# K for pairs of token tiles by seven half-size products, with phase 1 reordered

## The chip, the cores and the metric

The kernel runs on one core of one Trainium2 chip. The metric is device time in microseconds (us), the median of several runs. A core has five engines with a queue each: TensorE (PE, matmuls; its weight loads are shown as PEld), VectorE (DVE), ScalarE (ACT), GpSimd (POOL) and SyncE (SP, which here only issues transfers). Matmuls write to PSUM, a small memory of eight banks of 128 x 512 fp32; VectorE and ScalarE read it back. All data are fp32, and one fp32 product shows up as two matmul instructions in the profile.

## The reference

Two batches of 1024 tokens, model width 512. With `xn` the layer-normed input:

```python
Q = elu(xn @ wq.T + bq) + 1;  K = elu(xn @ wk.T + bk) + 1;  V = xn @ wv.T + bv    # 16 heads of 32
KV = K^T V per head;  K_sum = sum of K over the tokens
attn = (Q KV / (Q K_sum + 1e-8)) @ wo.T + bo
logits = xn @ W_router      # top 2 of 8 experts, weights from sigmoid scores
ffn = (silu(gate) * up) @ W_down, each with a shared and eight routed low-rank corrections
out = x + attn + ffn
```

## The kernel before, in words

Tokens lie in 16 tiles of 128 (`NTILE`), eight to a batch. A batch's `xnT` (features on partitions, tokens along the free axis) is kept in SBUF in four quarters: two halves of the features times two groups of 512 tokens. The program is written engine by engine in emission order: on TensorE, VectorE, ScalarE and GpSimd each instruction runs in the order in which the code emits it, so an instruction that waits holds up everything behind it on its engine. Transfers are issued from SP's queue, whose order the framework chooses.

Most large products use Winograd's form of Strassen's scheme: a 2 x 2 block product by seven half-size products, with sums of weight blocks and of token blocks made beforehand. For the queries (`query_unit`, from line 541) the sums of tokens come from `token_sums` (line 424: four subtractions of 1024 elements for a batch) and those of the weights from `query_weight_sums`.

Phase 1 is the loop from line 472, one tile a round. For tile i it:

- transposes the next tile's normed rows (`transpose_x`, line 262: four TensorE transposes, two ScalarE copies into `xnT`);
- norms the tile after that on VectorE (`norm`), from moments (`moments`, line 233) and a reciprocal standard deviation with one Newton step (`deviations`, line 239, with a Sqrt on ScalarE), and loads a new tile of x into a ring of four;
- computes K and the router's logits (`project_k`, line 271): four chunks of 128 features, each times two halves of the weights of 256 and 264 columns, plainly, no seven-product form. ScalarE copies the logits out; VectorE adds the bias and takes the minimum with 0, ScalarE takes the exp, VectorE finishes with `elu_k` (line 296);
- adds the previous tile's share to the Gram matrix (`accumulate`, line 299): four products xn^T K of 128 x 512 into four banks `pg` that stay open for a whole batch; GpSimd adds K into `ksum`.

The Gram matrix gives KV later, in `Finish` (line 309): copies out, `sums` (sums of `ksum`, and `ksr` from bank `pr`), `values` and `outputs`. For batch 0 it runs among the tiles of batch 1, for batch 1 as hooks of the first query unit. `route` (line 377) turns the logits of four tiles into expert weights. The four other banks rotate among `pt` and the two `pk`.

At the end of each group the query weight sums and the token sums are fed into VectorE's queue at fixed rounds (lines 522 to 528). `query_unit` computes seven products for two chunks with the banks `pqx`, `pqu`, `pqv`; ELU of a result is a VectorE operation, a relu and an exp on ScalarE, and a deferred add that `flush` emits. Phase 3 (from about 249 us) is the feed-forward part; `xdiff`, a difference of two halves of the low-rank activations, is made by GpSimd at its start (line 1255), and `inner_weight_sums` and `token_sums_23` are GpSimd's too.

Of the kernel before, what the change touches and what calls it, by code (L numbers as in the profile page):

```python
# [37 lines left out]
def layer_kernel(  # L38
# [56 lines left out]

    def by_chunk(w):
        return w.rearrange("(c p) n -> p c n", p=P)
# [42 lines left out]
    def load_x(i):  # L140
        x_sb[i] = x_ring[:, i % 4, :]
        nc.sync.dma_start(out=x_sb[i], in_=x[ts(i, P), :])
# [13 lines left out]
    for i, a in enumerate((a_gate, a_up)):  # L156
        nc.sync.dma_start(out=a_in[:, :, i, :], in_=by_chunk(a))
    ad_sb = const.tile([P, FULL + 1, LR], F32, name="ad_sb")
    nc.sync.dma_start(out=ad_sb[:, 0:FULL, :], in_=by_chunk(a_down[0 : FULL * P, :]))
    nc.sync.dma_start(out=ad_sb[0:REST, FULL, :], in_=a_down[RC, :])  # L160
# [52 lines left out]

    mv = p1.tile([P, NTILE, nc.vector.BN_AGGR_DIM], F32, name="mv")
# [5 lines left out]
    ps_pool = [pool(psum1, "ps1", bufs=4, space=PSUM)]  # L220
# [3 lines left out]
    def bank(name, shape=None):  # L224
        tag = next(tags) if tags else "ps"
        return ps_pool[0].tile(shape or [P, TB], F32, tag=tag, name=name)


    warm = bank("warm", [P, NC, P])
# [9 lines left out]
    def deviations(first, n):  # L239
        sl = slice(first, first + n)  # L240
        ve = p1w.tile([P, TPB], F32, tag="ve", name=f"ve{first}")[:, 0:n]
        nc.vector.tensor_scalar_add(ve, mv[:, sl, 1], LN_EPS)
        sd = p1w.tile([P, TPB], F32, tag="sd", name=f"sd{first}")[:, 0:n]
        nc.scalar.activation(sd, ve, AF.Sqrt)
        r0 = p1w.tile([P, TPB], F32, tag="r0", name=f"r0{first}")[:, 0:n]
        nc.vector.reciprocal(r0, sd)

        nt = p1w.tile([P, TPB], F32, tag="nt", name=f"nt{first}")[:, 0:n]
        nc.vector.tensor_mul(nt, r0, r0)
        nc.vector.tensor_mul(nt, nt, ve)  # L250
        nc.vector.tensor_scalar(nt, nt, -0.5, 1.5, ALU.mult, ALU.add)
        nc.vector.tensor_mul(rstd[:, sl], r0, nt)
# [3 lines left out]
    def norm(i):  # L256
        xns[i] = p1w.tile([P, D], F32, tag="xn", name=f"xn{i}", bufs=4)
        nc.vector.tensor_scalar(
            xns[i], x_sb[i], mv[:, i, 0:1], rstd[:, i : i + 1], ALU.subtract, ALU.mult
        )  # L260

    def transpose_x(i):
        pt = bank(f"pt{i}", [P, NC, P])
        for c in range(NC):
            nc.tensor.transpose(pt[:, c, :], xns[i][:, ts(c, P)], ident)
        for k in range(2):
            nc.scalar.copy(xnT[i // TPBATCH][k][:, :, ts(i % TPBATCH, P)], pt[:, 2 * k : 2 * k + 2, :])  # L267

    lg = {}

    def project_k(i, between=None):

        cols = ts(i % TPBATCH, P)
        pk = [bank(f"pk{i}_{s}", [P, HD + s * E]) for s in range(2)]
        for c in range(NC):
            if c == NC - 1 and between:
                between()
            for s in range(2):
                nc.tensor.matmul(  # L279
                    pk[s], xt(i // TPBATCH, c, cols), wk_sb[:, c, s * HD : (s + 1) * HD + s * E],  # L280
                    start=(c == 0), stop=(c == NC - 1),
                )
        g, t = i // TPB, i % TPB
        if t == 0:
            lg[g] = p2.tile([P, TPB, E], F32, tag="lg", name=f"lg{g}", bufs=2)
        nc.scalar.copy(lg[g][:, t, :], pk[1][:, HD:])

        kt = p1w.tile([P, D], F32, tag="kt", name=f"kt{i}", bufs=3)
        for s in range(2):
            nc.vector.tensor_add(kt[:, ts(s, HD)], pk[s][:, 0:HD], bk_sb[:, ts(s, HD)])  # L290
        ek = p1w.tile([P, D], F32, tag="ek", name=f"ek{i}")
        nc.vector.tensor_scalar_min(ek, kt, 0.0)
        nc.scalar.activation(ek, ek, AF.Exp)
        return kt, ek
# [4 lines left out]
    def accumulate(i, pg, ksum, xn, kt):  # L299

        j = i % TPBATCH
        if j == 0:
            nc.gpsimd.tensor_copy(ksum, kt)
        else:
            nc.gpsimd.tensor_add(ksum, ksum, kt)  # L305
        for m in range(NC):
            nc.tensor.matmul(pg[m], xn[:, ts(m, P)], kt, start=(j == 0), stop=(j == TPBATCH - 1))  # L307

    class Finish:
# [6 lines left out]
        def bank(self, name, shape=None):  # L316
            if self.b == 0:
                return bank(name, shape)
# [9 lines left out]
        def sums(self):  # L328
# [4 lines left out]
            pr = self.bank(f"pr{self.b}")  # L333
            nc.tensor.matmul(pr, ones, self.ksum, start=True, stop=True)
# [7 lines left out]

            self.ksr = p1.tile([P, NC, P], F32, tag="ksr", name=f"ksr{self.b}")
# [79 lines left out]

    def token_sums(b):
# [3 lines left out]
        ts_ = {1: b11, 2: b21, 3: b22}  # L428
        tsum.append(ts_)
        t12 = slot(10 if b == 0 else 9, [2, 2, TB], f"t12_{b}")  # L430
        tsum_pair.append(t12)
        ts_[5], ts_[6] = t12[:, 0], t12[:, 1]
        nc.vector.tensor_sub(ts_[5], b12, b11)
        yield
        nc.vector.tensor_sub(ts_[6], b22, ts_[5])
        yield
        t34 = slot(11, [2, 2, TB], "t34_0") if b == 0 else tsp.tile([P, 2, 2, TB], F32, tag="t2", name="t34_1")
        ts_[7], ts_[4] = t34[:, 0], t34[:, 1]
        nc.vector.tensor_sub(ts_[7], b22, b12)
        yield  # L440
        nc.vector.tensor_sub(ts_[4], b21, ts_[6])
# [20 lines left out]
    for i in range(2):  # L462
        moments(i, 1)
        deviations(i, 1)
        norm(i)
        load_x(i + 4)
    transpose_x(0)
    wq_sums, sums0, sums1 = query_weight_sums(), token_sums(0), token_sums(1)
    late = None
    fin = []  # L470
    ws = {}
    for i in range(NTILE):
        if i == 0:
            wv_sb = slot(4, [NC, D], "wv_sb")
            nc.sync.dma_start(out=wv_sb, in_=by_chunk(wvT))
        if i == 1:
            wo_sb = slot(5, [NC, D], "wo_sb")
            nc.sync.dma_start(out=wo_sb, in_=by_chunk(woT))
        if i == 2:
            wq_sb = slot(6, [NC, D], "wq_sb")  # L480
            nc.sync.dma_start(out=wq_sb, in_=by_chunk(wqT))
        if 0 < i < NTILE - 1:
            transpose_x(i + 1)
        if i == 0:
            moments(2, 1)
            deviations(2, 1)
        if i + 2 < NTILE:
            norm(i + 2)
        if i + 6 < NTILE:
            load_x(i + 6)  # L490
        kt, ek = project_k(i, (lambda: transpose_x(1)) if i == 0 else None)
        if i == 0:
            moments(3, 1)
        more = i % 2 == 1 and i + 3 < NTILE
        if more:
            moments(i + 3, 2)
        elu_k(kt, ek)
        if more:
            deviations(i + 3, 2)
        if i == 0:  # L500
            deviations(3, 1)
        n = i // TPB - 1
        if i % TPB == 0 and n >= 0:
            ws[n] = route(n)
        if i == 1:
            gather_factors()
            make_spread()
        t = i - TPBATCH
        if t == 3:
            fin[0].outputs((0, 1))  # L510
        if t == 4:
            fin[0].outputs((2, 3))
        if late is not None:
            accumulate(*late)
            if t == 0:
                fin.append(Finish(0, late[1], late[2]))
                fin[0].copies()
# [1008 lines left out]
```

## Time and profile before

| | us |
|---|---|
| median of 3 runs | 747.81 (746.48 to 747.92) |
| the profiled execution | 746.78 |
| its span, first to last instruction | 745.0 |
| TensorE busy | 733.7 |
| VectorE busy | 465.7 |
| ScalarE busy | 201.0 |
| GpSimd busy | 159.1 |
| phase 1, from the first K product to the first query product | 8.2 to 132.4 |
| first query unit | 132.4 to 169.7 |

A row of a timeline has the start, the length, the engine, the line of the kernel, the operation, what it writes and reads (buffer numbers left out), the shape, and the number of instructions that were merged; in brackets the idle time before it and what ended it. A length is that of the whole row: instructions of one engine overlap a little, so the distance from start to start is the better measure of what one costs. The mean granted TensorE clock was 0.999 of full speed.

### The profile page before, as it was taken

How to read it: one execution, taken by the hardware profiler on the slowest of the kernel's cores; microseconds unless marked ns; L12 is line 12 of the kernel's file. 1: busy time of each engine (PE TensorE's matmuls, PEld its weight loads, DVE VectorE, ACT ScalarE, POOL GpSimd, SP SyncE). 2: the span in 40 equal slices, each digit the busy share in tenths (PEclk: the TensorE clock that was granted, in tenths of full speed). 3: DMA queues.
4: the chain of work that ended last, by engine and by line, in shares of the span. 5: the costliest groups of instructions: out<-in, count | busy, mean ns of one | idle time of the engine just before them, and what ended most of it. 6: DMA issues, size and time to landing. Idle time of an engine off the chain costs nothing.

```text
span 745.0 us, 8741 instructions
## 1 busy us (share of the span) xinstructions
PE 733.7 (98%) x3106; PEld 494.8 (66%) x3106; DVE 465.7 (63%) x967; ACT 201.0 (27%) x432; POOL 159.1 (21%) x201
## 2 busy tenths in 40 slices
PE   8999999999999999999999999999999999999997
PEld 6666666454333566666566666666788888888886
DVE  5666665455677788878888888878952602703303
ACT  4445352533333333333333343243000000000000
POOL 3211212012000790311212213524601003101001
PEclk9999999999999999999999999999999999999999
DMA  9811001007313101211210210352465316323001
GB/s 232 231 29 43 15 0 58 0 1 185 121 29 126 33 4 57 84 33 57 86 53 33 85 58 29 127 183 97 162 189 196 125 45 209 124 68 112 19 1 57
DMA packets 52733, 63.29 MB, mean 85 GB/s; under 512 B 9425, under 2 KB 39505, under 8 KB 52434
## 3 DMA queue, kind: packets, MB, share of 16 engines
q1 hardware_dynamic: 52018, 62.46, 26.6%
q10 hardware_dynamic: 672, 0.28, 0.3%
q8 instruction: 24, 0.39, 0.2%
q14 instruction: 19, 0.16, 0.1%
HBM read 40.97 MB, written 21.76 MB: 84 GB/s over the span
## 4 chain that ended last, share of the span: by engine, by line
PE 87%; DVE 8%; ACT 2%; issue 1%; DMA 0%; POOL 0%; DVEq 0%; ACTq 0%
PE po L1383 25%; PE ab L956 15%; PE b L1016 7%; PE pk L279 7%; PE pg L307 6%; PE pqu L559 3%; PE ph L1406 3%; PE x L956 2%; PE pqv L559 2%; PE pxa L638 2%; PE pr L850 2%; PE b L1011 2%; DVE r L1038 2%; PE x L1011 1%; PE pv L355 1%
## 5 line engine op out<-in xcount | busy, mean ns | idle before, releaser
L1383 PE MATMUL po<-wd,f 128*128 128x256 f32 x560 | 122.5, 380 | 0.3 <-DVE xr L1452 0.2
L1383 PEld LDWEIGHTS po<-wd,f 128*128 128x128 f32 x560 | 106.0, 190 | 16.4 <-issue 2.1
L1016 PE MATMUL b<-t,w 128*128 128x512 f32 x160 | 83.2, 602 | 0.0
L279 PE MATMUL pk<-wk_sb,xnT 128*128 128x256 f32 (+1 forms) x256 | 59.3, 384 | 1.4 <-ACT xnT L267 1.4
L307 PE MATMUL pg<-kt,xn 128*128 128x512 f32 x128 | 57.5, 592 | 0.0
L1413 DVE TENSOR_TENSOR had<-ph,wT 64x256 f32<-64x256 f32 x8 | 3.4, 422 | 80.7 <-PE ph L1406 80.5
L279 PEld LDWEIGHTS pk<-wk_sb,xnT 128*128 128x128 f32 x256 | 47.4, 190 | 8.8 <-ACT xnT L267 2.1
L1430 ACT COPY a<-po 128x512 f32<-128x512 f32 x4 | 2.3, 585 | 185.1 <-PE po L1383 185.1
L1383 PE MATMUL po<-kvo,f 128*128 128x256 f32 x224 | 49.4, 381 | 0.0
L1038 POOL TENSOR_TENSOR r<-r,r 128x512 f32<-128x512 f32 x20 | 30.2, 1531 | 83.0 <-DVE t L1038 83.0
L1383 PEld LDWEIGHTS po<-kvo,f 128*128 128x128 f32 x224 | 42.3, 190 | 7.1 <-issue 1.2
L956 PE MATMUL ab<-ti,wi 128*128 128x256 f32 x180 | 45.4, 379 | 0.0
L956 PEld LDWEIGHTS ab<-ti,w 128*128 128x128 f32 x140 | 25.2, 189 | 29.7 <-DVE r L984 9.3
L1038 DVE TENSOR_TENSOR r<-r,r 128x512 f32<-128x512 f32 x60 | 44.1, 776 | 0.0
L956 PEld LDWEIGHTS ab<-ti,wi 128*128 128x128 f32 x180 | 34.2, 190 | 13.1 <-issue 4.8
L956 PE MATMUL ab<-ti,w 128*128 128x256 f32 x140 | 41.2, 388 | 0.7 <-DVE r L984 0.4
L307 PEld LDWEIGHTS pg<-kt,xn 128*128 128x128 f32 x128 | 24.4, 190 | 25.2 <-issue 23.6
L989 ACT COPY r<-ab 128x256 f32<-128x256 f32 x50 | 18.6, 372 | 71.8 <-PE ab L956 71.8
L305 POOL TENSOR_TENSOR ksum<-ksum,kt 128x512 f32<-128x512 f32 x14 | 19.9, 1423 | 77.4 <-DVE kt L297 47.7
L1016 PEld LDWEIGHTS b<-t,w 128*128 128x128 f32 x160 | 29.3, 190 | 10.4 <-issue 5.9
L966 ACT COPY r<-ab 128x256 f32<-128x256 f32 x50 | 18.6, 373 | 49.1 <-PE ab L956 46.9
L984 DVE TENSOR_TENSOR r<-r,ab 128x256 f32<-128x256 f32 x50 | 20.9, 418 | 17.2 <-ACT r L981 16.7
(240 smaller groups left out, 1259.2 us busy)
## 6 DMA issues: line engine op xcount, KB each, us to landing
h_dram<-h SPq DMA_DIRECT2D x40, 256.0 KB
f<-h_dram SPq DMA_DIRECT2D x20, 512.0 KB
x_ring<-in_x_dram SPq DMA_DIRECT2D x16, 256.0 KB
q_dram<-qt SPq DMA_DIRECT2D x16, 256.0 KB
f<-q_dram SPq DMA_DIRECT2D x8, 512.0 KB
xr<-in_x_dram SPq DMA_DIRECT2D x8, 512.0 KB
out_dram<-xr SPq DMA_DIRECT2D x16, 256.0 KB
w<-in_w_gate_dram SPq DMA_DIRECT2D x10, 256.0 KB
```

The lines of the kernel that those rows point to most:

```text
L279: nc.tensor.matmul(pk[s], xt(i // TPBATCH, c, cols), wk_sb[:, c, s * HD : (s + 1) * HD + s * E], start=(c == 0), stop=(c == NC - 1),)
L305: nc.gpsimd.tensor_add(ksum, ksum, kt)
L307: nc.tensor.matmul(pg[m], xn[:, ts(m, P)], kt, start=(j == 0), stop=(j == TPBATCH - 1))
L559: nc.tensor.matmul(banks[c], wqs[p][:, k, ts(c, P)], tsum[b][p][:, k, :], start=(start and k == 0), stop=(k == 1), skip_group_check=True,)
L956: nc.tensor.matmul(out, w, t, start=start, stop=True, skip_group_check=True)
L966: nc.scalar.copy(self.r[0][:, H0], self.ua)
L984: nc.vector.tensor_add(self.r[1][:, H1], self.r[1][:, H1], self.lo)
L1011: nc.tensor.matmul(banks[m], bgu_sb[rows, cols], act[rows, :], start=starts[m], stop=True, skip_group_check=True)
L1016: nc.tensor.matmul(pb[m], ws[m][:, A_OF[p], ts(k, P)], tsum[b][p][:, k, :], start=start, stop=True, skip_group_check=True)
L1038: eng.tensor_add(to[m], t[m], v[m])
L1383: nc.tensor.matmul(ps[p][:, q, :], lhsT, rhs, start=start, stop=stop, skip_group_check=True)
L1406: nc.tensor.matmul(ph[g * ER : (g + 1) * ER, :], a, f[:, g, :], start=(n == 0), stop=(n == len(chunks) - 1), skip_group_check=True,)
```

## The change

Tiles are taken in pairs: tile t of token group 0 and tile t of token group 1 of a batch (`TILES`). The first pair is still computed with `project_k`; the seven others with `k_pair`, where the two tiles are the two token blocks, the two halves of the features the inner blocks, and the two halves of K's columns the outer blocks. Seven products of 128 x 256 (or 264, with the logits' columns) over 256 features go into three banks, `ua`, `x` and `lo`; the bank `ua` is written by product 1 and then added to by products 6, 5 and 3, and VectorE reads it between them. Each product is two fp32 matmuls. The four sums of K's weights are made by GpSimd at the start (`key_weight_sums`), the four sums of tokens by VectorE for each pair (`pair_token_steps`); for batch 0 they are written where the query unit expects `token_sums(0)`, which goes away.

Around it: the Gram products, transposes, norms and moments are interleaved with the products in a new order; the Newton step works column by column; each Sqrt is followed by a dummy Exp; the logits are copied by VectorE; the loads of `a_in`, `ad_sb`, `wq`, `wv` and `wo` are held back by a small VectorE memset (`hold`) until given places in the order; factor and spread copies on GpSimd come in pair 3; routing comes in pair 7 and in the first query unit; in `query_unit` the copies of u2 come before the ELU of the first results; `xdiff` is made before phase 3.

```diff
+    TILES = [b * TPBATCH + g * TPB + t for b in range(NBATCH) for t in range(TPB) for g in range(2)]
...
+    def hold(v):
+        nc.vector.memset(v, 0.0)
...
-    for i, a in enumerate((a_gate, a_up)):
-        nc.sync.dma_start(out=a_in[:, :, i, :], in_=by_chunk(a))
+    def load_factors():
+        hold(a_in[:, 0, 0, 0:1])
+        for i, a in enumerate((a_gate, a_up)):
+            nc.sync.dma_start(out=a_in[:, :, i, :], in_=by_chunk(a))
+        hold(ad_sb[:, 0, 0:1])
...
+    def variances(first, n):
...
         nc.scalar.activation(sd, ve, AF.Sqrt)
+        if first > 2:
+            nc.scalar.activation(idle[:, 1:2], idle[:, 0:1], AF.Exp)
...
-        nc.vector.tensor_mul(nt, r0, r0)
-        nc.vector.tensor_mul(nt, nt, ve)
+        cols = [slice(k, k + 1) for k in range(n)]
+        for c in cols:
+            nc.vector.tensor_scalar(nt[:, c], r0[:, c], r0[:, c], ve[:, c], ALU.mult, ALU.mult)
         nc.vector.tensor_scalar(nt, nt, -0.5, 1.5, ALU.mult, ALU.add)
-        nc.vector.tensor_mul(rstd[:, sl], r0, nt)
+        for k, c in enumerate(cols):
+            nc.vector.tensor_scalar_mul(rstd[:, first + k : first + k + 1], nt[:, c], r0[:, c])
...
+    def key_weight_sums():
+        a11, a12 = (wk_of[0, k][:, :, 0:HD] for k in range(2))
+        a21, a22 = wk_of[1, 0], wk_of[1, 1]
+        s1, s2, s3, s4 = (wks[:, k, :, 0:HD] for k in range(4))
+        nc.gpsimd.tensor_add(s1, a21, a22)
+        nc.gpsimd.tensor_sub(s2, s1, a11)
+        nc.gpsimd.tensor_sub(s3, a11, a21)
+        nc.gpsimd.tensor_sub(s4, a12, s2)
...
+    def pair_token_steps(m):
...
+        nc.vector.tensor_sub(t34[:, 0], b22, b12)
+        yield
+        nc.vector.tensor_sub(t12[:, 0], b12, b11)
+        nc.vector.tensor_sub(t12[:, 1], b22, t12[:, 0])
+        nc.vector.tensor_sub(t34[:, 1], b21, t12[:, 1])
...
+    def add_keys(late):
+        (na, _, ksum, ka), (_, _, _, kb) = late
+        if na % TPBATCH == 0:
+            nc.gpsimd.tensor_add(ksum, ka, kb)
+        else:
+            for kt in (kb, ka):
+                nc.gpsimd.tensor_add(ksum, ksum, kt)
...
+    def k_pair(m, late, hooks={}):
...
+        product(2, x_, True)
+        product(7, lo, True)
+        product(1, ua, True)
...
+        if m == 1:
+            moments(4, 2)
+            variances(4, 2)
+        nc.vector.tensor_copy(la, ua[:, HD:])
+        nc.vector.tensor_add(ka[:, HI], ua[:, 0:HD], bk_sb[:, HI])
+        nc.vector.tensor_add(ka[:, HI], ka[:, HI], x_[:, 0:HD])
+        nc.vector.tensor_add(la, la, x_[:, HD:])
+        if m == 1:
+            reciprocals()
+        norms()
+        at("n")
+        add_keys(late)
+        if m > 1:
+            accumulate(*l_a)
+        else:
+            accumulate(*l_b, ms=range(3))
+        product(6, ua)
+        nc.vector.tensor_add(ka[:, LO], ua[:, 0:HD], bk_sb[:, LO])
+        at("a")
+        if ahead:
+            transpose_x(2 * m + 2)
+        accumulate(*l_b, ms=range(2) if m > 1 else ())
+        more = 2 * m + 4 < NTILE
+        if more:
+            moments(2 * m + 4, 2)
+            variances(2 * m + 4, 2)
+        product(5, ua)
+        nc.vector.tensor_add(kb[:, LO], ua[:, 0:HD], bk_sb[:, LO])
+        nc.vector.tensor_add(kb[:, LO], kb[:, LO], lo)
+        if ahead:
+            transpose_x(2 * m + 3)
+        accumulate(*l_b, ms=range(2, 4) if m > 1 else (3,))
+        at("b")
+        if m > 1 and ahead:
+            pair_token_sums(m + 1)
+        product(4, lo)
+        product(3, ua)
+        nc.vector.tensor_add(ka[:, LO], ka[:, LO], lo)
+        sums = pair_token_steps(2) if m == 1 else iter(())
+        next(sums, None)
+        ea = elu_min(ka, f"ek{na}") if m > 1 else None
+        nc.vector.tensor_add(kb[:, HI], ua[:, 0:HD], bk_sb[:, HI])
+        nc.vector.tensor_copy(lb, ua[:, HD:])
+        ea = ea or elu_min(ka, f"ek{na}")
+        list(sums)
+        elu_k(ka, ea)
+        eb = elu_min(kb, f"ek{nb}")
+        if more:
+            reciprocals()
+        elu_k(kb, eb)
...
+    hooks = {
+        (1, "b"): [lambda: load_weights(wq_sb, wqT)],
+        (2, "n"): [lambda: next(wq_sums), load_factors],
+        (2, "b"): [lambda: next(wq_sums), lambda: load_weights(wv_sb, wvT)],
+        (3, "n"): [lambda: next(wq_sums), lambda: next(wq_sums)],
+        (3, "b"): [lambda: load_weights(wo_sb, woT), lambda: pair_token_sums(0), gather_factors, make_spread],
+        (4, "b"): [lambda: fin.append(Finish(0, pg, ksum)), lambda: fin[0].copies()],
+        (5, "a"): [lambda: fin[0].sums(), lambda: fin[0].chunk_sums()],
+        (6, "a"): [lambda: fin[0].values()],
+        (6, "b"): [lambda: fin[0].outputs((0,))],
+        (7, "a"): [lambda: routed(0), lambda: fin[0].outputs((1,))],
+        (7, "b"): [lambda: fin[0].outputs((2, 3))],
+    }
...
+        if m == 0:
...
+            ka = project_k(0, [[(0, "lo"), (1, "ua")]], lambda: transpose_x(1))
+            variances(3, 1)
+            key_weight_sums()
+            ea = elu_min(ka, "ek0")
+            reciprocals()
+            norm(3)
+            load_x(7)
+            kb = project_k(1, [[(1, "x"), (0, "pt")]])
+            transpose_x(2, "lo")
+            elu_k(ka, ea)
+            eb = elu_min(kb, "ek1")
+            transpose_x(3, "ua")
+            pair_token_sums(1)
+            elu_k(kb, eb)
...
-        for c in two:
-            elu(c, 0)
         hook("P1")
         product(6, up, start=False)
         u2 = [q[c + NPQ, 0] for c in two]
         for c in two:
             nc.scalar.copy(u2[c], up[c])
-        flush()
+        for c in two:
+            elu(c, 0)
...
-        ws[3] = route(3)
-        accumulate(*late)
-        fin.append(Finish(1, late[1], late[2]))
+        add_keys(late)
+        for args in late:
+            accumulate(*args)
+        for n in (1, 2):
+            routed(n)
+        fin.append(Finish(1, pg, ksum))
...
+        nc.gpsimd.tensor_sub(xdiff[b], xa[b][:, 0:TB], xa[b][:, TB:BT])
```

## The prediction

> **What bounds the kernel now.** I read the page first (busy shares, the chain that ended last), then the timeline of each engine over the first 190 us, where the edits lie, and last the waits.
>
> ```profile
> PE 733.7 (98%) x3106; PEld 494.8 (66%) x3106; DVE 465.7 (63%) x967; ACT 201.0 (27%) x432; POOL 159.1 (21%) x201
> PE 87%; DVE 8%; ACT 2%; issue 1%; DMA 0%; POOL 0%; DVEq 0%; ACTq 0%
> ```
>
> TensorE is busy all the time, so a saved matmul is saved time only as long as the next one finds its operands and its bank ready. TensorE's timeline shows the old rhythm and the two holes that matter here.
>
> ```profile
> 49.37 0.60 PE L265 MATMUL pt<-ident,xn 128*128 128x128 f32 x4
> 49.81 3.67 PE L279 MATMUL pk<-wk_sb,xnT 128*128 128x256 f32 x16
> 53.32 3.60 PE L307 MATMUL pg<-kt,xn 128*128 128x512 f32 x8
> 56.75 0.60 PE L265 MATMUL pt<-ident,xn 128*128 128x128 f32 x4
> ...
> 82.28 3.34 PE L279 MATMUL pk<-wk_sb,xnT 128*128 128x264 f32 x14 [0.60 <-ACT xnT L267]
> ...
> 148.89 3.70 PE L559 MATMUL pqu<-t,wq_sums 128*128 128x512 f32 x8 [0.90 <-ACT qt L595]
> ...
> 722.16 12.36 PE L1383 MATMUL po<-kvo,f 128*128 128x256 f32 x56
> ```
>
> From start to start: four transposes 0.44, K of one tile 3.51 (16 instructions, two for each fp32 product), its share of the Gram 3.43 (8 instructions, 0.43 each): 7.38 us a tile, without idle. A 256-wide instruction takes 0.218 (12.2 us over 56, L1383).
>
> What could stop the new order is VectorE, which must empty the bank between products, and who holds VectorE up. Two timelines side by side, VectorE:
>
> ```profile
> 54.34 0.54 DVE L258 TENSOR_SCALAR xn<-x_ring,mv,rstd 128x512 f32<-128x512 f32 x1
> 59.25 1.49 DVE L258 TENSOR_SCALAR xn<-x_ring,mv,rstd 128x512 f32<-128x512 f32 x1
> 64.52 0.17 DVE L246 RECIPROCAL r<-sd 128x2 f32<-128x2 f32 x1 [0.27 <-ACT sd L244]
> 64.72 0.88 DVE L249 TENSOR_TENSOR nt<-r 128x2 f32<-128x2 f32 x1
> ```
>
> and GpSimd:
>
> ```profile
> 58.88 1.58 POOL L305 TENSOR_TENSOR ksum<-ksum,kt 128x512 f32<-128x512 f32 x1 [5.67 <-DVE kt L297]
> 64.32 1.27 POOL L305 TENSOR_TENSOR ksum<-ksum,kt 128x512 f32<-128x512 f32 x1 [3.86 <-DVE ve L242]
> ```
>
> The same norm takes 0.54 alone and 1.49 beside a GpSimd add; both delayed operations end just after that add does. The reciprocal beside it is not delayed. Last, ScalarE's table loads:
>
> ```profile
> 22.02 1.28 ACT L244 ACT_TABLE_LOAD   x1 [1.68 <-DVE ve L242]
> ...
> 33.20 1.28 ACT L244 ACT_TABLE_LOAD   x1
> 34.77 0.20 ACT L244 ACTIVATE sd<-ve 128x2 f32<-128x2 f32 x1 [0.28 <-DVE ve L242]
> ```
>
> A Sqrt needs a load of 1.28. Sometimes it starts before the Sqrt's input is there (33.20), sometimes only after (22.02).
>
> **What it removes from TensorE.** Pair 0 is still computed plainly. Seven pairs go from 32 instructions to 28, and the 264-wide ones stay 128 in number, so 7 x 4 = 28 instructions of width 256 go: 28 x 0.218 = 6.1 us, all on the bounding engine. A new pair is 6.15 (28 products) + 6.87 (16 Gram) + 0.87 (8 transposes) = 13.9 us on TensorE, against 14.8.
>
> The first two norms lose one small VectorE operation each (0.195 from start to start in the first timeline microseconds): TensorE starts 0.2 earlier. The 0.60 at 82.28 came from ScalarE's table loads ahead of a transpose copy in an order that is gone. The 0.90 at 148.89 came from relu and exp standing ahead of the u2 copies; now the copies come first, and the two later routings fit in VectorE's idle 5.2 us before 141.75 plus the 3.4 us of the extra Gram tile. Without that cover the 0.9 comes back. Together 1.7.
>
> **What it adds: the loop of a pair.** The copies of the logits move from ScalarE to VectorE, the four long token sums of batch 0 (1.22 each, L433 to L441) become four short ones in every pair. I lay VectorE's queue out in emission order. Step A is the add that empties ua after product 6; step B is the add that empties lo after product 4.
>
> From B to A: minimum 0.37, kb's add and the logits' copy wait beside it for the exp (0.46 + 0.03 + 0.63 after B), ELU of ka 0.6, minimum 0.4, six small reciprocal operations 0.9, ELU of kb 0.7, then next pair: copy, two adds, small add 1.0 (PSUM adds 0.42). At kb's ELU GpSimd starts its two key adds of 1.27; each norm waits for one of them, as at 59.25: 2.6 us instead of 0.9 for the two norms; then A 0.42. Sum 7.6 us.
>
> From A to B: two moments 1.7 (start to start of L236 and L237 here), variance 0.2, Sqrt 0.2, the dummy Exp's load 1.28 and 0.2, two transpose copies 0.63, four pair sums of 256 elements 1.6 (0.34 to 0.45 each, as L730 to L732), B 0.42. Sum 6.1 us, if the Sqrt's own load runs ahead of its input.
>
> 13.7 us against TensorE's 13.9: it fits, with 0.2 to spare. Every stall is therefore what comes on top. On TensorE, product 5 is due 2.15 us after product 6 ends and needs A; the next pair's product 7 is due 7.83 after it and needs B; behind either waits the whole of TensorE.
>
> Pair 2 starts late (below), and hooks add a query weight sum (0.6) and the holds of the factor loads: A at +2.35, B at +8.45: stalls 0.25 + 0.37. Pair 3 adds two weight sums (1.2): A at +2.75 costs 0.65, B 0.57; its sums of pair 0 (1.6) hide behind the copies but for 0.2. Pair 4: none. Pair 5: pr goes into the transposes' bank and its reader must finish first: 0.35. Pairs 6 and 7 have no moments; the routing (3.9 us at 43.42 to 47.49) stands ahead of steps that product 4 needs only 6.9 us later. Sum 2.2. Bounds: 0 if the norms are not held up, 5 if each pair stalled 0.8.
>
> **The start.** Four key weight sums (GpSimd 1.27 each) begin when wk has landed. The transfers up to it are 2.05 MB, which the stretches show moved by about 9.3 us. So they run until 15, and norm 2 (ready at 11.2), ka's minimum and norm 3 each wait for one. Here the Trainium skill (SBUF — State Buffer, Who interferes with whom; VectorE: DVE Perf Modes, What auto-detection actually checks) weighs against the change and limits the loss at once: two-input and two-port VectorE operations wait for a GpSimd operation that reads SBUF, as the rows show, but a two-port mode needs an even dimension, so one-column operations would not. No row of before has one beside a GpSimd add. By the rule norm 2 ends near 12.5; if one-column operations waited too, near 15, and the sum grows 2.5. I take the rule, since the reciprocal's row (0.17) points its way.
>
> By hand from there: product K of tile 1 ends 15.5; transpose 3 waits for norm 3 until 16.8 (0.85), the Gram of tile 0 for its ELU until 18.05 (0.85). In pair 1 product 5 waits 0.1 and product 4 waits 0.5, as the moments stand ahead of the add that empties lo; at pair 2 the Gram waits 0.6 for ka. Sum 2.9, between 1 (GpSimd out of the way) and 5.5.
>
> **Moves costed at nothing.** The five holds are VectorE memsets of the smallest kind (0.15, in VectorE's waits, or counted above). SP's queue: the x tiles no longer stand behind a_in; wq is issued about 31 and read about 41, and 1 MB at 385 GB/s (windows 20 to 26) plus issue is under 6 us; late, it would hold pair 2's norms' successors one for one. wv and wo have tens of microseconds. Factor and spread copies on GpSimd (4.8 us) move to pair 3: copies did not delay the norm at 11.76 (0.55 beside them). The two xdiff subtractions (3.4) leave a stretch where TensorE idled 0.24: at best that.
>
> **Sum.** -6.1 - 0.2 - 1.5 + 2.2 + 2.9 = -2.7 us. The profiled execution took 746.78 (span 745.0 and 1.8 around it), so 744.1 like it; it lies 1.0 under the median of 747.81, and beside that median I expect **745.1 us**. What a measurement tells from no change is 0.2%, 1.5 us: 746.3 and 749.3 are the borders.
>
> **Rivals.** *All stalls covered* (chance 0.22): if wk lands late enough or the adds of GpSimd fall between the norms, the start costs 1 and the pairs 0.3: -6.5, so 741.3. For it: VectorE is busy only 62 of 98 us in this phase before. Against: its order is fixed, and the loop has 0.2 us to spare.
>
> *The Sqrt's load waits for its input* (0.15), as at 15.50 and 22.02, not as in the five later pairs. Place: between A and B of every pair with moments, 1 to 5. Price: 1.28 in the loop, 15.0 against 13.9; worked through: pair 1 +1.0, pair 2 +1.3, pair 3 +1.1, pair 4 +1.1, pair 5 +0.4 = 4.9, so 745.1 + 4.9 = 750.0, slower. Since the loop has only 0.2 to spare, each pair pays what exceeds that; the gain is gone when 2.7 of these 4.9 us are paid, a load that waits some 0.7 us in each pair.
>
> *The gain is eaten at the start* (0.13): one-column operations wait for GpSimd as well: +2.5, so 747.6, no change. Against: the reciprocal at 64.52.
>
> **Numbers.** The likeliest case has 0.45, and its own range is 743 to 747 (the bounds of start and pairs at once are rarer); 0.05 is left for what I don't see. Faster: 0.36 of it, 0.22, and 0.04 of the rest: 0.62; same 0.20; slower 0.18. The range takes in the covered case and the waiting load: 741.0 to 750.2.
>
> **What would show it.** K's products: 228 instructions instead of 256, of 0.38 each. TensorE's waits: products 5 and 7 of pairs 2 and 3 for VectorE, 0.3 to 0.7 each; transposes and Gram before 20 us; none at pqu for the u2 copies. VectorE: the norms at 1.0 to 1.5 each from pair 2 on. ScalarE: table loads of L244's successor starting ahead of the variance. I am wrong if TensorE waits over 1 us in pairs 4 or 5, if the first Gram starts before 17 or after 20 us, or if a hole opens in the query unit.

## The result, and the profile after

The changed kernel takes **743.94 us** (median of 6 runs, 743.5 to 745.15) beside 747.36 of the kernel before in the same session (6 runs): ratio **0.9958 [0.9945, 0.9971]**, 3.4 us less. I had said 745.1, between 741.0 and 750.2. Its profiled execution took 744.27, with a span of 742.5; my sum, made against the profiled execution of before, was 744.1. So the total is right, in part by luck: two errors cancel, and without one small step that I had priced at nothing most of the gain would not have reached the end.

The page after, with busy time and the chain that ended last:

```profile
PE 730.5 (98%) x3078; PEld 489.6 (66%) x3078; DVE 484.6 (65%) x1044; ACT 195.9 (26%) x421; POOL 161.0 (22%) x206
PE 80%; DVE 12%; POOL 3%; issue 2%; DMA 2%; ACT 1%; SPq 0%; DVEq 0%; POOLq 0%; ACTq 0%
```

TensorE issues 3078 instructions instead of 3106: the 28 are gone. But the chain now runs through VectorE for 12% of the span (8% before) and through GpSimd for 3% (0% before). The other engines were pulled closer to the edge. TensorE's timeline, pair 3 and the start of pair 4:

```profile
53.80 1.03 PE L424 MATMUL kua<-wk_sums,t 128*128 128x256 f32 x4
...
57.20 1.16 PE L424 MATMUL kua<-wk_sums,t 128*128 128x264 f32 x4 [0.22 <-DVE kt L455]
...
63.35 1.13 PE L424 MATMUL klo<-wk_sums,t 128*128 128x256 f32 x4 [0.19 <-DVE kt L475]
...
68.75 1.03 PE L424 MATMUL kua<-wk_sums,t 128*128 128x256 f32 x4
```

From product 6 to the next pair's product 6 this takes 14.95 us, with two waits for VectorE: at product 5 (57.20) and at the next product 7 (63.35). In pair 4 the same distance is 13.84, the 13.9 of my working without a stall. The holes of before at 82.28 (0.60) and 148.89 (0.90) have no counterpart.

What the edits did to the moments at which TensorE reaches four places (the same kernel, profiled once more in the last experiments, gives the first four within 0.1 us):

| TensorE starts | before | after | earlier by |
|---|---|---|---|
| `pw` (first row after the first query unit) | 171.68 | 167.16 | 4.5 |
| first `ab` of the feed-forward part | 249.57 | 244.82 | 4.75 |
| `y` of its first unit | 275.64 | 270.72 | 4.9 |
| `y` of its second unit | 302.61 | 299.06 | 3.55 |
| end of the span | 745.0 | 742.5 | 2.5 |

So phase 1 and the first query unit gave 4.5 us, well over my 2.7; at `y` of the first unit the lead is 4.9, and 2.4 us of that went again. TensorE's timeline after shows where 1.25 of it went:

```profile
270.72 1.02 PE L1223 MATMUL y<-xa,bgu_sb 64*128 64x512 f32 x4
272.13 0.70 PE L1168 MATMUL ab<-ti,w 128*128 128x256 f32 x2 [0.39 <-DVE r L1196]
...
274.55 1.12 PE L1228 MATMUL b<-t,w 128*128 128x512 f32 x2 [0.42 <-DVE r L1250]
276.11 0.70 PE L1168 MATMUL ab<-t,w 128*128 128x256 f32 x2 [0.43 <-DVE r L1204]
```

Before, the first of these waits was 0.24, and the other two were not there:

```profile
276.91 0.70 PE L956 MATMUL ab<-ti,w 128*128 128x256 f32 x2 [0.24 <-DVE r L984]
```

They are named for VectorE. VectorE itself waits for GpSimd there. Two rows of VectorE's timeline of after:

```profile
273.81 0.69 DVE L1250 TENSOR_TENSOR r<-r,b 128x512 f32<-128x512 f32 x1 [1.73 <-POOL r L1250]
275.03 0.69 DVE L1250 TENSOR_TENSOR r<-r,b 128x512 f32<-128x512 f32 x1 [0.54 <-POOL r L1250]
```

And GpSimd's timeline of after shows why it is late:

```profile
250.17 0.46 POOL L1142 TENSOR_TENSOR wi<-w 128x128 f32<-128x128 f32 x1 [3.56 <-DMA r_dram<-hr]
...
270.83 1.71 POOL L1098 TENSOR_TENSOR ti<-xnT,ti 128x512 f32<-128x512 f32 x1
272.51 2.49 POOL L1250 TENSOR_TENSOR r<-r,r 128x512 f32<-128x512 f32 x2
```

It ends its token sums `ti` at 272.5, as it did before (272.25), although TensorE arrives 4.9 us earlier. In between it stood idle for 3.56 us until a store of `hr` had landed. In GpSimd's timeline of before the first such sum starts at 246.91, ahead of TensorE's first `ab` at 249.57:

```profile
246.91 0.54 POOL L930 TENSOR_TENSOR wi<-w 128x128 f32<-128x128 f32 x1 [70.55 <-DMA sb<-in_b_gate_dram]
...
272.25 3.39 POOL L1257 TENSOR_TENSOR xdiff<-xa 128x512 f32<-128x512 f32 x2
```

Most of the rest was lost near 633: from the first `po` to the end this profile takes 220.0 us and that of before 219.2, with a wait of `po` for `xr` of 0.78 that before doesn't have. In the second profile of the same kernel that wait is not there either, the stretch takes 219.2 and the span is 741.6: that one is a matter of the single execution.

### The profile page after: what moved, and what is told of

Its sections match the earlier page's. It is cut to its first block, busy times and chain, and to the rows that moved or that the text cites. A ratio compares the mean times of both kernels' runs of the same rounds, so it can differ in the third digit from the quotient of the medians.

```text
span 742.5 us, 8737 instructions
## 1 busy us (share of the span) xinstructions
PE 730.5 (98%) x3078; PEld 489.6 (66%) x3078; DVE 484.6 (65%) x1044; ACT 195.9 (26%) x421; POOL 161.0 (22%) x206
## 4 chain that ended last, share of the span: by engine, by line
PE 80%; DVE 12%; POOL 3%; issue 2%; DMA 2%; ACT 1%; SPq 0%; DVEq 0%; POOLq 0%; ACTq 0%
PE po L1586 25%; PE ab L1168 14%; PE b L1228 6%; PE pg L395 5%; PE pqu L761 4%; PE ph L1609 3%; PE kua L424 2%; PE x L1168 2%; POOL ti L1098 2%; PE pxa L840 2%; PE pqv L761 2%; PE b L1223 2%; PE pr L1062 1%; PE klo L424 1%; PE x L1223 1%
## 5 line engine op out<-in xcount | busy, mean ns | idle before, releaser
L1196 DVE TENSOR_TENSOR r<-r,ab 128x256 f32<-128x256 f32 x50 | 20.9, 419 | 20.2 <-ACT r L1193 19.8
L404 POOL TENSOR_TENSOR ksum<-ksum,kt 128x512 f32<-128x512 f32 x12 | 15.8, 1315 | 72.7 <-DVE lg L441 43.3
L1634 POOL TENSOR_TENSOR xr<-xr,a 128x512 f32<-128x512 f32 x4 | 5.1, 1273 | 121.1 <-ACT a L1633 81.0
L1204 DVE TENSOR_TENSOR r<-r,ab 128x256 f32<-128x256 f32 x50 | 20.9, 418 | 15.4 <-ACT r L1201 15.1
```

Source lines behind the costliest of these rows:

```text
L1196: nc.vector.tensor_add(self.r[1][:, H1], self.r[1][:, H1], self.lo)
L1204: nc.vector.tensor_add(self.r[1][:, H0], self.r[1][:, H0], self.lo)
```

## Experiments

Each kernel is the changed kernel with one edit, unless it is said otherwise. The kernel before took 748.17, 748.25 and 748.24 on the three chips used, so the medians can be set side by side. The unaltered changed kernel is the measure:

> The changed kernel unaltered, as the measure for the single edits, which all ran in another session than it did. If sessions don't differ, the ratio is 0.9958 again (745.0 beside 748.2), and the three single edits that gave 0.993 are each worth 2 us. If it is 0.993, none of them is worth anything that can be measured, and the two that gave 0.996 (ELU first; key weight sums late) cost 2 us each. By the traces I expect about 0.994 to 0.995: the edits move their milestones by 0.7 to 1.1 us.

Measured: 743.93 us (743.34 to 744.79), ratio 0.9943 [0.993, 0.9955]. That is 4.3 less than the kernel before; the result had 3.4. All differences below are against it. A single one under about 1 us rests on its trace and not on its median.

### The xdiff step undone

```diff
-    token_diffs(0, "xd")
...
-    token_diffs(1, "den")
...
+        if j == 0:
+            first["2c"] = [lambda: (token_diffs(0, "xd"), token_diffs(1, "den"))]
         unit(j, 0, first)
```

> The two xdiff subtractions go back to where they stood before, behind the token sums of GpSimd in the first feed-forward unit. My prediction gave this step at best 0.24 us. If GpSimd's queue is what sets the pace at 272 to 277, as the three waits there suggest, TensorE now comes 4.9 us earlier to a queue that is 2.6 to 3.4 us longer: y waits for xdiff from 270.7 until 274 to 276, and the time grows by 2.5 to 4 us. If the waits there come from VectorE's own queue, the cost is the 0.24 of before, and under 0.5.

Measured: **747.58 us**, 3.65 more; ratio to before 0.9987 [0.9979, 0.9996]. TensorE's and GpSimd's timelines of this kernel:

```profile
273.90 2.04 PE L1222 MATMUL b<-xdiff,bgu_sb 64*128 64x512 f32 x4 [3.97 <-POOL xdiff L971]
```

```profile
272.59 2.47 POOL L971 TENSOR_TENSOR xdiff<-xa 128x512 f32<-128x512 f32 x2
```

The first query product (126.33) and the first `ab` (244.92) stand as in the unaltered kernel. Then TensorE reaches GpSimd's queue and stands for 4 us, and the two products behind the wait take about twice their time (2.04 and 1.86); the waits that follow in the unaltered kernel fall away in return. Without this step the whole rewriting of phase 1 would have brought 0.7 us instead of 4.3. In the kernel before the same order had cost next to nothing, because TensorE came 4.9 us later: its trace has no wait for `xdiff`. The step alone, in the kernel before, was not run.

### GpSimd's idle time filled

```diff
-    list(inner_weight_sums(nc.gpsimd, 0, (2,)))
     list(token_sums_23(0, slot(4, [2, 4, TH], "ti23_0")))
+    list(inner_weight_sums(nc.gpsimd, 0, (2,)))
```

> At the start of phase 3 GpSimd makes the token sums of products 2 and 3 of batch 0 before the weight sums of product 2, whose tile waits until about 250 us for a transfer out of r; the work is the same. Theory that the new waits of TensorE between 272 and 277 (1.2 us, for VectorE, which waits for GpSimd's add r<-r,r) come from GpSimd idling 3.6 us at that transfer: GpSimd's sums end near 269 instead of 272.5, the three waits go, -1.0 to -1.2 against the changed kernel, 742.8, ratio 0.9943. Rival that GpSimd is held up by VectorE's two-input operations and not by the transfer: its sums end at about the same time and the waits stay, no change.

Measured: 742.60 us (1.3 less), span 740.6. GpSimd now starts the token sums at 246.59 without a wait and is done 4 us earlier:

```profile
246.59 1.59 POOL L1098 TENSOR_TENSOR ti<-xnT 128x512 f32<-128x512 f32 x1
...
270.05 2.81 POOL L1250 TENSOR_TENSOR r<-r,r 128x512 f32<-128x512 f32 x2 [1.63 <-ACT r L1189]
```

All three waits at 272 to 277 are gone. A new one opens earlier: at 262.74 a product waits 0.79 for VectorE's add into `t`, since two adds ahead of that one take 3.40 instead of 1.85 beside GpSimd's sums. So `y` of the first unit is 1.06 later and that of the second, 297.99, is 1.0 earlier. So GpSimd's late start was the cause of those waits. Why its weight sums of product 2 wait for the store of `hr` is not shown; that they now share memory with it was not tried.

### How much room the pair loop has

> Eight more dummy Exps on one column after the dummy Exp of each of the five later Sqrts (pairs 1 to 5), 0.1 to 0.2 each, so ScalarE gives the second transpose's copies 0.8 to 1.6 later; no other work. Theory that the chain from the add after product 6 to the add after product 4 has next to nothing to spare: the delay comes out in pairs 1, 2 and 3 in full and in 4 and 5 in half, for 1.2 of delay about 4 x 1.2 = +4.4 us against the changed kernel, 748.3, ratio 1.002, with waits of TensorE for VectorE at product 7 or the next product 1 of every pair. Rival that the chain has slack in every pair: under +1.

```diff
         nc.scalar.activation(idle[:, 1:2], idle[:, 0:1], AF.Exp)
+            if first > 5:
+                for _ in range(8):
+                    nc.scalar.activation(idle[:, 1:2], idle[:, 0:1], AF.Exp)
```

Measured: 752.88 us, 8.95 more, twice what I expected; ratio to before 1.0054 [1.0039, 1.0068]. The eight take 1.84 us on ScalarE, 9.2 in five pairs, and the first query product starts 9.55 later. TensorE's waits, and the longest of them in its timeline:

```profile
engine line waited for: us in total, times, longest us
PE klo L427 <- DVE kt L478: 5.5, 4, 2.1
```

```profile
68.88 2.07 PE L427 MATMUL klo<-wk_sums,t 128*128 128x256 f32 x4 [2.06 <-DVE kt L478]
```

Product 7 waits for the add B in the four later pairs, and in the first for a token sum that stands just ahead of it (1.1). From product 6 to product 6, pairs 1 to 3 grow by 1.8 each: there the stretch from A to B has no room, and what is added to it is paid in full. Pairs 4 and 5 grow by 1.2 and 1.3, so they had some 0.6 to spare. Pair 3 grows by another 1.7, because the eight instructions behind the wait of 2.06 run slower (2.07 and 1.84 instead of 1.13 and 1.12). That the total comes near 9.2 is luck.

The other direction, the dummy Exp's load taken out of that stretch:

```diff
             transpose_x(2 * m + 3)
+        if more:
+            nc.scalar.activation(idle[:, 1:2], idle[:, 0:1], AF.Exp)
```

(and it is left out of `variances` for these pairs)

> In pairs 1 to 5 the dummy Exp after a Sqrt is moved behind the copies of the second transpose. The stretch from A to B of my loop then loses a table load of 1.28 and the Exp's 0.2, so product 7 of the next pair no longer waits in pair 3. My theory (the stalls of pairs 2 and 3 are VectorE's loop, with ScalarE's table loads in it): the wait at klo goes, first query product 0.6 to 0.9 earlier, near 125.4. Rival (the loop is held up by the norms beside GpSimd's adds alone, ScalarE has slack): wait at klo unchanged at 0.2, query product at 126.2; or the Exp's load now stands ahead of ELU's exp and a wait for it opens at kua or pg, 0.5 in each pair.

Measured: 742.59 us (1.3 less), first query product at 125.31 (0.87 earlier), second `y` at 298.14 (0.87 earlier). ScalarE's timeline in pair 3:

```profile
58.12 0.20 ACT L264 ACTIVATE sd<-ve 128x2 f32<-128x2 f32 x1 [0.95 <-DVE ve L262]
58.27 0.65 ACT L302 COPY xnT<-pt 128x256 f32<-128x256 f32 x2
58.93 1.28 ACT L470 ACT_TABLE_LOAD   x1
60.22 0.20 ACT L470 ACTIVATE idle<-idle 128x1 f32<-128x1 f32 x1
```

The copies follow the Sqrt at once. The load (now at 58.93) and its Exp end at 60.4, and ScalarE then has 2.45 us before ELU's exp. The wait at product 7 is gone, and so is the one at product 5 in pair 3. The rival, a load that is late for the exp, didn't happen.

Two more edits take other work out of the loop. The key adds on GpSimd, twelve of fourteen left out:

```diff
-            for kt in (kb, ka):
-                nc.gpsimd.tensor_add(ksum, ksum, kt)
+            pass
```

> GpSimd's additions of the keys into their sum are left out for all pairs but the first of each batch (12 of 14 additions of 512 elements); the sum of keys then covers one pair only, so the attention's denominators and the bias part of the values are those of fewer tokens. Theory that the norms wait for these additions: two norms take 1.0 instead of 2.25 us in pairs 2, 3 and 4, the add after product 6 comes 1.2 earlier, and the waits in pair 3 (0.4 at product 5, 0.4 at product 7 and its follower) and 2 (0.2) go: -0.8 to -1.1, 743.0, ratio 0.9945. Rival that the norms' length is free because TensorE waits for something else there: no change, and the waits at products 5 and 7 of pair 3 stay.

Measured: 742.85 us, first query product at 125.24, 0.94 earlier. The two norms of pair 3, 2.26 with the adds (53.14 in the changed kernel), in VectorE's timeline of this one:

```profile
52.80 1.00 DVE L292 TENSOR_SCALAR xn<-x_ring,mv,rstd 128x512 f32<-128x512 f32 x2
```

The adds hold up the norms by 1.26 us in pairs 2, 3 and 4 alike, but only where TensorE was waiting does that reach the time: 0.9, not three times 1.26. And the last two query weight sums, from pair 3 to pair 6:

```diff
-        (3, "n"): [lambda: next(wq_sums), lambda: next(wq_sums)],
+        (6, "n"): [lambda: next(wq_sums)],
+        (6, "b"): [lambda: next(wq_sums), lambda: fin[0].outputs((0,))],
```

> The last two query weight sums (0.6 each on VectorE) move from pair 3 to pair 6, where there are no moments. Theory that they push the add after product 6 of pair 3 beyond its due time: the waits of pair 3 at products 5 and 7 (0.4 each) shrink to under 0.2 together, -0.7 against the changed kernel, 743.2, ratio 0.9949. Rival that pair 3 waits because of pair sums 0, the hook that follows: the wait at product 7 stays, -0.3 at most.

Measured: 742.97 us, first query product at 125.54 (0.64 earlier), no wait at product 7, product 5 of pair 3 without one. Three different edits, on ScalarE, GpSimd and VectorE, take away the same waits of pair 3 and give 0.6 to 0.9 each: the stalls are VectorE's queue, and there is not much more to fetch from it (they are 1.3 us in all pairs together).

### The saved matmuls given back

```diff
         product(2, x_, True)
+        product(2, x_, True)
```

> Product 2 of each of the seven pairs is issued twice into its bank (the second starts the sum afresh, so the result stays): 28 instructions more of width 264, 28 x 0.22 = 6.2 us of TensorE work, as many as the change took away, and nothing else moves. Theory that TensorE sets the pace and the saved matmuls are the gain: 6.2 less the waits for VectorE that the longer pair hides (0.4 at product 7 of pair 3, 0.4 at product 5, 0.2 in pair 2), so +5.2 against the changed kernel, 749, ratio to before 1.002. Rival that VectorE's queue sets the pace of a pair and the gain lies in the query unit: less than +3, ratio under 1.000.

Measured: 748.32 us; ratio to before 1.0002 [0.9994, 1.001]. With 28 instructions more the kernel is 4.4 us slower, not 6.2, and the first query product is 4.8 later. The difference can be placed: in the unaltered kernel pairs 2 and 3 lose 0.2 and 1.0 us to stalls (distances from start to start, above the pace of each width), and with the longer pairs that is gone; the first K product was 0.2 earlier in this execution. So the seven products are the source of the gain: without them everything else in the change brings nothing (ratio 1.0002), and with them but without the xdiff step 0.7 us is left. Each needs the other. 4.4 to 4.8 us is what the saved instructions are worth in this order.

### The query unit and the start

ELU of the first results ahead of the u2 copies again:

```diff
+        for c in two:
+            elu(c, 0)
         hook("P1")
         product(6, up, start=False)
         ...
-        for c in two:
-            elu(c, 0)
```

> In the query unit the ELU of the first results stands ahead of the u2 copies again, as in the kernel before (both units). Theory that this order was the 0.9 us hole of the first unit: TensorE waits for the u2 copies before product 5, +0.5 to +0.9 against the changed kernel, 744.7, ratio 0.997. Rival that the hole went because of the second Gram tile or the moved routing: no wait there and no change.

Measured: 745.59 us, 1.7 more. TensorE's timeline has the old hole back, a little wider than before (0.90):

```profile
146.48 3.70 PE L761 MATMUL pqu<-t,wq_sums 128*128 128x512 f32 x8 [1.11 <-ACT qt L797]
```

The four sums of K's weights held back until norm 3 is done:

```diff
             variances(3, 1)
-            key_weight_sums()
             ea = elu_min(ka, "ek0")
             reciprocals()
             norm(3)
+            nc.gpsimd.tensor_copy(idle[:, 0:1], xns[3][:, 0:1])
+            key_weight_sums()
```

> A copy of one column of norm 3's result on GpSimd stands ahead of the key weight sums, so these start after norm 3 instead of at 10.2 us. Theory that they hold up norm 2 (1.47 us) and ka's minimum (1.13) and with them the first Gram product: both at 0.55 and 0.43, norm 3 at about 15.2 instead of 16.6, the Gram of tile 0 starts 1.0 to 1.5 earlier, and part of it is lost again as the sums now run beside the pair sums and product 7 waits for the third: -0.5 to -1.2, 743.0, ratio 0.9946. Rival that the start hangs on the x tiles, the transposes' copies or the slow first matmuls: the Gram starts at 18.4 as now, no change.

Measured: 745.55 us, 1.6 more. VectorE's timeline of this kernel:

```profile
15.55 0.55 DVE L292 TENSOR_SCALAR xn<-x_ring,mv,rstd 128x512 f32<-128x512 f32 x1
...
18.20 1.49 DVE L332 TENSOR_SCALAR ek<-kt 128x512 f32<-128x512 f32 x1
20.91 1.40 DVE L384 TENSOR_TENSOR t<-xnT,xnT 128x256 f32<-128x256 f32 x1 [1.23 <-ACT xnT L302]
```

Norm 3 is at 15.55, instead of 16.57 in the result's profile, and the first Gram only 0.1 earlier (18.33). The second profile of the unaltered kernel says the same without any edit: there GpSimd's sums start 0.35 later (10.52), hold up neither norm 2 nor the minimum (0.55 and 0.43), norm 3 is at 15.68, and the first Gram at 18.41. So the first Gram doesn't hang on this delay alone. With the edit the sums then hold up the minimum of kb (1.49 instead of 0.42) and the first token sum (1.40 instead of 0.42), and the transposes of pair 1 wait 1.24 us for their norm (29.35). The delay was not removed, only moved to a place where nothing covers it.

### The end, and all that helped

```diff
-            for t in kvo_next:
-                block_diffs(t)
...
         nc.gpsimd.tensor_add(x2[:, :, d1], x2[:, :, d1], u2)
+        if u == 1:
+            for t in kvo:
+                block_diffs(t)
```

> In the output phase GpSimd takes the differences of the second batch's kvo blocks after its two adds to xr instead of before them. Theory that TensorE's wait at 633 (0.8, for VectorE's xr adds, which wait for GpSimd's, which stand behind a transfer of kvo): the wait goes, -0.8 to -1.0, 743.0, ratio 0.9947. Rival that xr is late for another reason (its own results): the wait stays, no change.

Measured: 742.92 us (1.0 less). The wait of `po` for `xr` is gone, but the 0.8 that I set out from was that of one execution: the unaltered kernel's second profile has only 0.19. The second `y` stands at 299.07, as in the result's profile. From the first `po` to the end this kernel takes 218.5 us; twelve profiles without the edit take 219.2 to 220.0. So the traces give it 0.7.

Token sums first on GpSimd, query weight sums in pair 6, block differences later, dummy Exp behind the copies, together:

> Four edits at once: token sums of the first half before the weight sums of product 2 on GpSimd; two query weight sums moved from pair 3 to pair 6; block differences of kvo after the xr adds; dummy Exp behind the copies. If each acts on its own wait, the sum of what their traces showed: pair loop 0.7 (the second and the fourth act on the same wait), feed-forward start 1.1, end 0.7: some 2.5 us under the unaltered kernel of the same call. If the last queue on the way to the end takes it back, as it did with the change itself, under 1.

Measured: **740.59 us** (740.45 to 742.29), ratio to before **0.9904 [0.9888, 0.9919]**, 3.3 under the changed kernel; its slowest run is under the fastest of either kernel. First query product 125.25, second `y` 296.95, span 738.8. In the pair loop the two edits act on the same wait (125.31 with one of them alone). The gain of the pair loop (0.9) and that of GpSimd's order (1.0) add up, since 299.01 became 296.95; the end adds 0.7, since from the first `po` it takes 218.5 here too.

## Why the prediction was right, and where it was not

**Matmuls saved, -6.1.** Right: 228 K instructions instead of 256 at the pace of 0.217, and pair 4 takes 13.84. Given back alone they cost 4.4 to 4.8, since longer pairs hide stalls.

**The start, +2.9.** Right in size; in place only where TensorE runs at its full pace. In the second profile of the changed kernel, measured as distance from start to start above the pace of each width, the stalls from 8.2 to the Gram of pair 2 are 1.4 + 0.5 + 0.3 + 0.2 + 0.3, with 0.4 in slower products behind them: 3.1, before 0.3, net 2.8. The 1.4 are the first K products, which ran in part at half pace (last section); I had not thought of that, and my 0.85 at transpose 3 is not there. In the two kernels in which they ran at full pace (GpSimd's order, ELU first) TensorE does wait for norm 3 at transpose 3, 0.93 and 0.91, and the stalls are 3.1 again. The 0.85 at the Gram was 0.5. The two delays lie beside each other: where VectorE's was absent, the first Gram came no earlier. The 0.2 us of earlier start did not come: the first K product is at 8.24, before at 8.21.

**The rule for one-column operations.** Right. GpSimd's sums of weights run from 10.17 to 15.4 in after; the first of them, and VectorE beside it:

```profile
10.17 1.27 POOL L318 TENSOR_TENSOR wk_sums<-wk_sb 128x512 f32<-128x512 f32 x1 [7.13 <-DMA wk_sb<-in_wkT_dram]
```

```profile
10.85 0.27 DVE L278 TENSOR_SCALAR nt<-r,ve 128x1 f32<-128x1 f32 x1
...
11.60 1.47 DVE L292 TENSOR_SCALAR xn<-x_ring,mv,rstd 128x512 f32<-128x512 f32 x1
```

At 15.82, where GpSimd has only its last small copies, the same one-column operation takes 0.27 as well; the norm takes 0.55 at 16.57 and 1.47 here. Norm 2 ends at 13.07, near the 12.5 that I took and not near 15. The rival *the gain is eaten at the start* falls with it. My reading of the rule was too short, though: the Trainium skill (VectorE: DVE Perf Modes, What auto-detection actually checks) asks for dimensions that are even or that are equal in source and destination, so it did not settle the case of one column. The rows do, for these operations.

**The pair loop, +2.2.** The mechanism is right, the sum too large: 1.3, by the same distances. Pair 2 lost 0.2 instead of 0.62, pair 3 1.0 instead of 1.22, pair 4 nothing, pair 5 0.1 instead of 0.35. The terms that I listed for the loop add up to 7.7 and 6.2, so to 14.0 and not to 13.7, which would leave nothing to spare. In the trace VectorE needs 13.5 from A of pair 3 to A of pair 4 (56.74 to 70.26), beside TensorE's 13.84: a margin of 0.3, near the 0.2 that I had, but by a sum that was wrong.

**The waiting load, 750.0.** It fell in the trace. ScalarE's timeline of after:

```profile
24.13 1.28 ACT L264 ACT_TABLE_LOAD   x1 [4.21 <-DVE ve L262]
...
55.97 1.28 ACT L264 ACT_TABLE_LOAD   x1
59.00 0.21 ACT L264 ACTIVATE sd<-ve 128x2 f32<-128x2 f32 x1 [1.74 <-DVE ve L262]
```

Only the load of pair 1 waited (24.13); the five later ones ran ahead of their input, as here by 1.74 us. But the rival's price was sound. By what the pairs paid for 1.84 us each in the delay experiment, 1.28 would cost 1.28 in three pairs and 0.7 in two, 5.2 in all (an estimate, without slower products behind the waits): near my 4.9, and the change would have been a loss.

**Holes of before, -1.5.** Too small. The 0.60 and 0.90 are gone, and a wait of 0.56 (`psa` for VectorE's `qt`) that I had not counted went with them. With the slower products after each they cost 0.9, 1.2 and 0.8; 0.2 of that is left in the new kernel, so 2.7 went. Undoing the order of the u2 copies costs 1.7 us, so their cover is real. Together, -6.1 + 2.8 + 1.3 - 2.7 = -4.7, and at `pw` the second profile is 4.6 earlier than before.

**Moves costed at nothing: this is the step that failed.** I gave the xdiff subtractions "at best" 0.24, the idle time of TensorE in their stretch before (276.91 above). That reads a deadline as if it stayed where it was. TensorE came 4.9 us earlier to a GpSimd queue that ended at the same moment, and the step was worth 3.65. The same blindness hid what was left: three waits of 1.25 in sum, because GpSimd stood idle for a store ahead of its sums. My sum carried the gain of phase 1 to the end unchanged; in truth 4.5 to 4.9 came out of phase 1 and the query unit, and over 1 was lost at GpSimd. The two errors cancel in 744.1; that the total fits is luck. The other moves were free: the five holds took 0.06 each, and `wq`, held until 31.23, kept nobody waiting. None of my three signs of being wrong came: no wait over 1 us in pairs 4 and 5, the first Gram at 18.44, no hole in the query unit.

## What to carry to other kernels

When TensorE is made faster in one stage, look at each later place where another engine's queue has a fixed moment, and ask how late TensorE came to it before; a step that is worth nothing today may decide over most of the gain tomorrow. Compare a second profile of the same kernel before a difference of 1 us at one row is put down to an edit: here norm 3 moved by 0.9 with no edit at all. In a loop that only just closes, price every operation in it fully, and look for what can stand outside it, such as a table load that may as well follow the copies. Delays that lie beside each other are not fetched by removing one.

## What the runs showed of the hardware

**Half pace of TensorE at the start.** The first twelve K instructions, TensorE's timeline of the changed kernel and of the one with GpSimd's order changed:

```profile
8.24 3.90 PE L356 MATMUL pk<-wk_sb,xnT 128*128 128x256 f32 x12 [0.46 <-ACT xnT L302]
```

```profile
8.18 2.90 PE L356 MATMUL pk<-wk_sb,xnT 128*128 128x256 f32 x12 [0.78 <-ACT xnT L302]
```

The code of this stretch is the same. In the first kernel the instructions start 0.42 to 0.59 apart until 10.1 and then mostly 0.22, in the second 0.22 from the second one on. Over fourteen profiles (the kernel before among them) the twelve took 2.90 three times and 3.9 to 4.6 eleven times. In seven of the eleven the granted clock falls to 0.50 in one of the stretches 8.2 to 10.2 and 10.2 to 12.2. In the four others, the changed kernel's own two profiles among them, it reads 1.00 although the four transposes ahead are slow as well (1.1 instead of 0.6): at the start a reading of 1.00 doesn't prove full pace. The Trainium skill (TensorE: Matmul & The Clock Gate, What's actually happening) describes a gate that halves the pace until TensorE has been busy for a window, with a phase that differs from run to run; the doubled distances and the clock of 0.50 agree with that, the length of the window no run here shows. It cost little: the first Gram starts at 18.45 and 18.52 where the changed order ran at full pace, at 18.33 to 18.73 elsewhere.

**Half pace after a long wait.** After the wait of 3.97 us (the xdiff step undone) eight instructions took 2.04 and 1.86 instead of 1.13 and 1.02, with a granted clock of 0.53 from 273.9 to 277.5. After the wait of 2.06 (the delay in the pair loop) eight took 2.07 and 1.84 instead of 1.13 and 1.12, with 0.53 from 68.8 to 72.4. After a wait of 1.75 in the same kernel the next four took 1.13. So a long wait cost about 1.7 us more than its length.

**A load without a pause behind it.** A table load takes 1.28, and the Sqrt behind it starts 0.01 later (24.13 + 1.28, then 25.42).
